# A transformer block on one core: who rotates the first batch's queries and keys

## The chip, the core and the metric

The kernel runs on one core of a Trainium2 chip. The core has a matrix engine (TensorE, PE in the profile; PEld is its weight load), three engines for elementwise work (VectorE or DVE, ScalarE or ACT, GpSimd or POOL), and SyncE (SP), which here issues almost all DMAs. The engines run side by side and wait for each other on semaphores. Each executes its own instructions strictly in the order in which the program holds them. The metric is the device time of one execution in microseconds (us): the median of three runs.

## What is computed

The input is x of 16 batches, 1024 tokens, 256 features. The reference, cut to what matters:

```python
xn = layernorm(x)
Q, K, V = xn @ Wq.T + bq, xn @ Wk.T + bk, xn @ Wv.T + bv      # 16 heads of 16
re, ro = xe * cos - xo * sin, xe * sin + xo * cos             # rotation of Q and K, even and odd columns
attn = softmax(where(causal, Q @ K.T / 4, -1e9)) @ V
h = square(relu(xn @ W_fc.T)); y = h @ W_proj.T
spikes = five steps of a threshold recurrence on y, their sum / 5
out = x + attn @ Wo.T + bo + spikes
```

Products are made from float16 pairs: each operand is split into a high part (a float16 copy) and a low part (what the copy lost, as float16), and a product is three matmuls (high x high, high x low, low x high; `three`, line 590).

## The kernel before, in words

**An order made by a planner.** Every step is announced with `op(engine, cost, when, what, reads, writes, ...)`. `Plan.order` (193 to 321) then plays an event simulation with the given costs and due times `when`: an idle engine takes the ready step that is due first. The resulting order is written down, engine by engine, and a chain of order dependencies fixes it. So a change of an estimated cost, an engine or a dependency in one place can move instructions anywhere later. A step may name other engines in `alt`: if it has been ready and untaken for PATIENCE (1.5 us), an idle engine of that list may take it. `held` names a ring of SBUF tiles (sizes in `BUFS`, line 86); a step is not taken before its tile is free.

**What runs over what.** Batches are 140 us of planned time apart and overlap. For each batch `norms` (595) normalizes the tokens, splits them and transposes them by DMA into xT; `rotated` (655) makes Q and K; `values` (744) makes V; for each of four groups of heads (64 units in all) `largest` (791) takes the row maxima of the scores (matmuls L803, maxima L819 and L837 on VectorE) and `weighted` (910) makes the scores again with the maximum as an extra row (L920), the exponential on ScalarE (L981), the causal mask on POOL (L938) and the product with V (L947); `forward` (1088) is the feed-forward half with its spikes (L1147, L1152) and `projected` (1039) the output. Feed-forward matmuls (L590, with `wfc` and `wproj`) can be placed between attention matmuls. Row-packed matmuls (L803, L920), column-packed ones (L947) and full ones (L590) are three modes between which the planner changes as seldom as its due times allow.

**The rotation, the place of the change.** `rotated` works in four tiles per batch, Q and K of each half of the tokens, each 128 partitions x 1024 float32 (an even and an odd half of 512). A tile passes through these steps:

- two products into PSUM, two biased copies into `r` (`qk`, ScalarE, L670; two buffers),
- `times_` with the sines into `ms`, `times_` with the cosines in place (L678), `added` (L686),
- a float16 copy by ScalarE into `qkhl` (L733), and `less`, the low part (L689),
- `stored`: two DMAs to scratch in DRAM (L693, L697).

`load_slots` later reads Q into `qS` and K into one of three fixed tiles, the slots `kS` (L783). The slots are filled once with a constant by POOL (`memset`, L1232) before the first K is loaded; that fill is made to wait for `st.ready[3]`, the low part of the first batch's last token tile.

The elementwise combinations of two tiles go through `combined` (381). It gives them to POOL, with ScalarE as an alternative where one exists. With `vector=True`, which the first batch's rotation and the low parts of its normalized x (L649) use, VectorE is an alternative without patience, and the estimate for it is 2.1 ns an element. In the first batch the rotation is announced in half tiles (`parts`, `each`), so that the two engines can share a tile.

Of the kernel before, what the change touches and what calls it, by code (L numbers as in the profile page):

```python
# [16 lines left out]
ALU = mybir.AluOpType  # L17
# [4 lines left out]
P = 128  # L22
# [60 lines left out]
Q0, Q1 = 0.1, 0.71  # L83
V0, V1 = 0.43, 0.96
SHARE = 0.5
BUFS = dict(w=5, xn=2, x=3, relu=2, ms=2, hT=3, avT=2, ahl=6)

# [9 lines left out]
FULL, ROWS, COLS = "full", "rows", "cols"  # L97
SWITCH = 100.0
PATIENCE = 1500.0
# [39 lines left out]


class Op:
    __slots__ = ("mode", "engine", "cost", "when", "what", "held", "waits", "then", "start", "early", "ready", "size", "alt", "name", "patience")


class Plan:
# [7 lines left out]
        self.ops, self.writer, self.readers = [], {}, {}  # L153

    def op(self, engine, cost, when, what, reads=(), writes=(), also=(), window=None, size=0.0,
           alt=(), mode=FULL, patience=PATIENCE):
        o = Op()
        o.mode = mode
        o.size, o.alt, o.patience = size, alt, patience
# [24 lines left out]
        for key in writes:  # L184
            k0 = key[0] if isinstance(key, tuple) else key
            if isinstance(k0, (Held, Bank)):
                o.name = k0.name
                break
        for tile_ in held:
            tile_.left += 1  # L190
        self.ops.append(o)

    def order(self):
# [71 lines left out]
        while events:  # L265
            now = events[0][0]
            while events and events[0][0] <= now:
                _, _, kind, o = heappop(events)
                if kind == 0:
                    heappush(queues[o.engine], (o.when, o))  # L270
                    if o.alt:
                        heappush(events, (now + o.patience, n, 3, o))
# [61 lines left out]
def move(nbytes):  # L334
    return nbytes / 360.0
# [23 lines left out]
def tile_block(ctx: ExitStack, tc, x, wqkv, bqk, bv, wo, bo, wfc, wproj, cos, sin, out):  # L359
# [31 lines left out]

    def copied(n, when, out, in_, reads, writes, scale=None):

# [201 lines left out]
    def norms(st, times):  # L595
# [36 lines left out]
        for n in range(NC // 2):  # L632
            i = n // (NC // 4)
            t = times[n]
            if n % (NC // 4) == 0:
                for c in range(HALF):
# [11 lines left out]
            combined(512, t - 2e3,  # L648
                   lambda e, xn=xn, hl=hl: e.tensor_tensor(  # L649
                       hl.t[:, :, 1], xn.t, hl.t[:, :, 0], ALU.subtract),  # L650
                   [xn, (hl, 0)], [(hl, 1)], 2.05, vector=b == 0)
            op("sp", dma(1), t, lambda n=n, hl=hl: turned(n, hl), [(hl, 0), (hl, 1)], [(xT, n)],
               size=2 * move(P * 4 * D * 2))

    def rotated(st, times):
# [16 lines left out]
                bias=bqk_sb[:, 2 * t + eo : 2 * t + eo + 1], scale=1.0 / WS,  # L672
            )


        def times_(engine, table, half, to, r, es):
            cols = slice(half * QB, (half + 1) * QB)
            engine.tensor_tensor(  # L678
                to.t[:, es], r.t[:, es],
                table[:, :, cols].broadcast_to([P, es.stop - es.start, QB]), ALU.mult,  # L680
            )

        def added(engine, r, ms, es):
            for e in range(es.start, es.stop):
                a, b = (r.t[:, e, :], ms.t[:, 1 - e, :])[:: 1 if e == 0 else -1]
                engine.tensor_tensor(r.t[:, e, :], a, b, (ALU.subtract, ALU.add)[e])  # L686

        def less(engine, t, r, hl, es):
            engine.tensor_tensor(hl.t[:, 1 - t, es], r.t[:, es], hl.t[:, t, es], ALU.subtract)  # L689

        def stored(t, half, hl):
            to = scr[b % 2][t][:, :, half * QB : (half + 1) * QB]
# [9 lines left out]
        for half in range(2):  # L702
            for t in range(2):
# [16 lines left out]
                def each(after, what, reads, to, mine, rate=2.27):  # L720
                    for es in parts:
                        own = [(to, e) for e in range(2)[es]]
                        combined(n, at + QD + after, lambda e, es=es: what(e, es),
                                 reads if mine is None else [*reads, *((r, e) for e in range(2)[es])],
                                 own, rate, vector=b == 0)
# [6 lines left out]
                op("act", act(1024), at + QD + 10e3,  # L732
                   lambda t=t, r=r, hl=hl: nc.scalar.copy(hl.t[:, t], r.t), both, [(hl, t, 0), (hl, t, 1)])  # L733
                for es in parts:
# [5 lines left out]
                stored_keys = [(hl, x, e) for x in range(2) for e in range(2)]  # L740
                op("sp", dma(2), at + QD + 13e3, lambda t=t, half=half, hl=hl: stored(t, half, hl),
                   stored_keys, [("scr", b % 2, t, half)], size=move(P * 6 * QB * 2))

    def values(st, times):
        b = st.b
# [475 lines left out]
    for b in range(B):  # L1221
# [5 lines left out]
        if b == 0:  # L1227

            w_fc, WFC = split_weights(wfc, F, "wfc", 2, START + 12e3, [st.ready[1]])
            w_proj, WPROJ = split_weights(wproj, D, "wproj", 2, START + 30e3, [st.ready[3]])  # L1230
            for i, t in enumerate(k_slots):
                op("pool", 1700, START + 40e3 + i, lambda t=t: nc.gpsimd.memset(t, SHIFT),  # L1232
                   [st.ready[3]], [("kS", i)])
        rotated(st, at["q", b])
        values(st, at["v", b])
        for g in range(NG):
# [76 lines left out]
```

## Time and profile before

| | |
|---|---|
| median of 3 runs | 2438.48 us (2437.65 to 2441.66) |
| the profiled execution | 2438.26 us, span of its instructions 2436.6 us |
| TensorE busy | 2356.5 us, 97% |
| VectorE, ScalarE, GpSimd busy | 82%, 76%, 74% |
| mean granted TensorE clock | 0.993 |
| data moved | 246 MB, 101 GB/s |

The span runs from the first to the last instruction. A time of an instruction is its own; an idle time in square brackets stands before it, with what ended it. Matmul ends are modelled, so how fast TensorE gets on is read from the starts. Names after an L are lines of the kernel before.

How the first batch's combinations are spread in the stretch from 20 to 60 us: POOL executes 16 of them in half tiles, VectorE 15, and POOL three fills of 1.8 us each.

### The profile page before, as it was taken

To read this page: it belongs to the slowest core of one execution; us is meant where nothing else is said; L and a number is where in the kernel's file an instruction comes from. 1 tells how busy PE (TensorE), PEld (TensorE's weight loads), DVE (VectorE), ACT (ScalarE), POOL (GpSimd) and SP (SyncE) were. 2 spreads that over 40 slices of the span, in tenths; PEclk is the share of its full clock that TensorE was granted. 3 is DMA by queue.
4 is the path that set the end of the run, shared out by engine and by line. 5 is a ranking of instruction groups with operands and counts; after the bars stand their busy time and mean duration, and the time that the engine had idled before them with its cause. 6 is when DMAs were issued, how large, how long until landed. Compare 5 with 4: busy or idle time off the path is not lost.

```text
span 2436.6 us, 59006 instructions
## 1 busy us (share of the span) xinstructions
PE 2356.5 (97%) x21060; PEld 1182.3 (49%) x21060; DVE 1987.8 (82%) x6065; ACT 1843.3 (76%) x3599; POOL 1806.9 (74%) x1922
## 2 busy tenths in 40 slices
PE   5999999999999999999999999999999999999997
PEld 3544444445445445454544445455454444544553
DVE  6888888887987879788788878877878887787882
ACT  5588778787778778777787777787877878777775
POOL 7877757778678877779778587776877858687553
PEclk8999999999999999999999999999999999999999
DMA  5442524433334344344342434233433242432221
GB/s 170 110 102 80 137 80 120 106 89 108 91 119 111 89 100 109 93 110 123 89 115 84 106 113 105 89 96 84 130 98 115 89 103 88 106 113 82 68 68 54
DMA packets 253935, 246.21 MB, mean 101 GB/s; under 512 B 108104, under 2 KB 207816, under 8 KB 253640
## 3 DMA queue, kind: packets, MB, share of 16 engines
q1 hardware_dynamic: 253504, 242.44, 36.2%
q8 instruction: 165, 2.70, 0.5%
q14 instruction: 130, 1.06, 0.2%
q10 hardware_dynamic: 136, 0.00, 0.0%
HBM read 122.82 MB, written 101.71 MB: 92 GB/s over the span
## 4 chain that ended last, share of the span: by engine, by line
PE 58%; DVE 7%; ACT 3%; issue 2%; DMA 1%; POOL 1%; SPq 0%; POOLq 0%; DVEq 0%; ACTq 0%
PE banks L590 27%; PE banks L947 14%; PE banks L920 8%; PE banks L803 8%; DVE junk L837 3%; ACT w L981 2%; DVE nm_sb L819 1%; DVE count L1152 1%; DVE nm_sb L837 1%; PE banks L1041 1%; PE banks L864 0%; ACT hT L1128 0%; POOL hT L1134 0%; DMA av_dram<-avT 0%; DMA inv<-inv 0%
## 5 line engine op out<-in xcount | busy, mean ns | idle before, releaser
L981 ACT ACTIVATE w<-banks 128x512 f32<-128x512 f32 (+1 forms) x2560 | 1246.6, 572 | 294.6 <-PE banks L920 280.5
L819 DVE TENSOR_REDUCE nm_sb<-banks 128x1 f32<-128x512 f32 x1024 | 642.6, 683 | 138.8 <-PE banks L803 137.6
L947 PE MATMUL banks<-w,v_sb 128*32 128x512 f32 (+3 forms) x6144 | 622.9, 494 | 3.6 <-DVE nm_sb L819 1.4
L938 POOL TENSOR_SCALAR_AFFINE_SELECT w<-w 128x256 f32<-128x256 f32 x1024 | 399.3, 408 | 286.9 <-ACT w L981 271.7
L837 DVE CUSTOM_DVE_ANT_0 junk<-banks,mask,nm_sb 128x256 bf16<-128x256 f32 (+3 forms) x1024 | 498.1, 547 | 99.0 <-PE banks L803 61.9
L837 DVE CUSTOM_DVE_ANT_0 junk<-banks,mask 128x256 bf16<-128x256 f32 (+3 forms) x1024 | 444.4, 486 | 64.0 <-PE banks L803 57.2
L920 PE MATMUL banks<-qS,kS 50*128 50x512 f16 (+3 forms) x3072 | 431.7, 328 | 9.6 <-DVE nm_sb L819 3.5
L803 PE MATMUL banks<-kS,qS 48*128 48x512 f16 (+3 forms) x3072 | 415.8, 326 | 9.5 <-DVE nm_sb L837 4.3
L590 PE MATMUL banks<-wproj_hi,hT 128*128 128x256 f16 x2048 | 383.4, 276 | 8.0 <-ACT relu L1123 6.5
L590 PE MATMUL banks<-xT,wfc_hi 128*128 128x256 f16 x2048 | 350.3, 273 | 6.6 <-ACT w L981 2.5
L590 PEld LDWEIGHTS <-hT 128*128 128x128 f16 x3072 | 282.8, 98 | 110.2 <-issue 74.5
L1130 POOL TENSOR_TENSOR relu<-relu 128x1024 f32<-128x1024 f32 x118 | 223.5, 1894 | 125.6 <-ACT hT L1128 125.1
L920 PEld LDWEIGHTS <-kS 50*128 50x128 f16 x3072 | 132.7, 94 | 314.3 <-issue 288.6
L590 PE MATMUL banks<-wproj_lo,hT 128*128 128x256 f16 x1024 | 281.2, 275 | 0.0
L590 PE MATMUL banks<-xT,wfc_lo 128*128 128x256 f16 x1024 | 279.0, 273 | 0.0
L1134 POOL TENSOR_TENSOR hT<-relu,hT 128x1024 f16<-128x1024 f32 x128 | 273.4, 2136 | 2.9 <-ACT relu L1132 0.9
L947 PEld LDWEIGHTS banks<-w,v_sb 128*32 128x32 f32 x6144 | 152.8, 108 | 245.7 <-issue 189.5
L803 PEld LDWEIGHTS <-qS 48*128 48x128 f16 x3072 | 135.7, 94 | 269.7 <-issue 233.5
L1123 ACT ACTIVATE relu<-banks 128x512 f32<-128x512 f32 x256 | 156.1, 610 | 113.9 <-PE banks L590 110.2
L590 PEld LDWEIGHTS <-wfc_hi 128*128 128x128 f16 x2048 | 185.2, 98 | 92.0 <-issue 70.5
L678 POOL TENSOR_TENSOR ms<-qk,sin_sb 128x1024 f32<-128x1024 f32 (+1 forms) x65 | 150.1, 2309 | 70.5 <-ACT qk L670 70.2
L1152 DVE SCALAR_TENSOR_TENSOR count<-banks,count 128x512 f16<-128x512 f32 x256 | 175.2, 684 | 3.6
(84 smaller groups left out, 2820.7 us busy)
## 6 DMA issues: line engine op xcount, KB each, us to landing
av_dram<-avT SPq DMA_DIRECT2D x128, 256.0 KB, 2.1
qS<-scr_q SPq DMA_DIRECT2D x128, 192.0 KB, 3.5
kS<-scr_k SPq DMA_DIRECT2D x128, 192.0 KB, 4.4
x<-in_x_dram SPq DMA_DIRECT2D x66, 256.0 KB, 3.2
scr_q<-qkhl SPq DMA_DIRECT2D x32, 512.0 KB, 3.1
scr_k<-qkhl SPq DMA_DIRECT2D x32, 512.0 KB, 3.0
av<-av_dram SPq DMA_DIRECT2D x64, 256.0 KB, 3.4
inv<-inv SPq DMA_DIRECT2D x64, 256.0 KB, 3.3
```

The source lines that it names most:

```text
L590: nc.tensor.matmul(out, lhsT=lhs[i], rhs=rhs[j], start=first and n == 0, stop=last and n == 2)
L803: nc.tensor.matmul(pts[two].t[:, at : at + w], lhsT=qS.t[r, h, c * P : (c + 1) * P], rhs=kS[r, h, k0 : k0 + w], start=True, stop=True,)
L819: lambda two=two, pt=pt: nc.vector.tensor_reduce(nm0[:, two, i, c : c + 1], pt.t, axis=AX.X, op=ALU.max),
L837: nc.vector.tensor_tensor_reduce(next(junk)[:, :w], pt.t[:, at : at + w], mask[:, QB - w :], scale=1.0, scalar=nm0[:, two, i, chunk] if pa ...
L920: nc.tensor.matmul(pts[two].t[:, at : at + n], lhsT=kS[r, i, j * P : (j + 1) * P], rhs=qS.t[r, i, qb * QB + off : (qb + 1) * QB], start=Tr ...
L938: nc.gpsimd.affine_select(out=d, in_=d, compare_op=ALU.is_ge, fill=0.0, base=0, pattern=[[0, 2], [1, P]], channel_multiplier=-1,)
L947: nc.tensor.matmul(pav.t[VT * h : VT * (h + 1), off:], lhsT=st.v[:, j, col : col + VT], rhs=ws[h % 2].t[:, h // 2, at : at + QB - off], st ...
L981: lambda n=n, two=two, pt=pt, w=w: nc.scalar.activation(w.t[:, two, :n], pt.t[:, :n], AF.Exp, scale=SCALE),
L1123: lambda r=r, ph=ph, pr=pr: nc.scalar.activation(r.t[:, 2 * pr : 2 * pr + 2].rearrange("p f t -> p (f t)"), ph.t, AF.Relu, scale=1.0 / WS),
L1130: combined(1024, when + 4e3, lambda e, r=r: e.tensor_tensor(r.t, r.t, r.t, ALU.mult), [], [(r, 0), (r, 1)], 1.75, lambda r=r: nc.scalar.ac ...
L1134: lambda e, r=r, hT=hT: e.tensor_tensor(hT.t[:, 1], r.t, hT.t[:, 0], ALU.subtract),
L1152: lambda step=step: nc.vector.scalar_tensor_tensor(flat(count), py.t, least[step], flat(count), ALU.is_gt, ALU.add),
```

## The change

- `combined` takes `vector` as a number. If it isn't 0, the step is VectorE's alone, with an estimate of 70 ns an instruction and 1.06 ns an element; there is no choice left to the planner, and the `patience` field goes.
- The first batch's rotation is announced in whole tiles like that of the others, and goes to VectorE: per tile one product with the sines (1024 elements), one with the cosines, two sums of 512, and one low part of 1024. The low parts of the first batch's normalized x go to VectorE too.
- `ms` loses its entry in `BUFS`, so its ring has one buffer instead of two, in all batches.
- The fill of K's slots waits for `st.ready[1]` instead of `st.ready[3]`: the low part of the second token tile, not of the fourth.

```diff
-BUFS = dict(w=5, xn=2, x=3, relu=2, ms=2, hT=3, avT=2, ahl=6)
+BUFS = dict(w=5, xn=2, x=3, relu=2, hT=3, avT=2, ahl=6)
...
-    def combined(n, when, what, reads, writes, rate=2.27, scalar=None, vector=False):
-        alt, patience = [], PATIENCE
-        if scalar is not None:
-            alt = [("act", act(n) + 35, scalar)]
+    def combined(n, when, what, reads, writes, rate=2.27, scalar=None, vector=0):
         if vector:
-            alt, patience = [("dve", dve(n, 2.1), lambda: what(nc.vector))], 0.0
-        op("pool", pool_(n, rate), when, lambda: what(nc.gpsimd), reads, writes, alt=alt,
-           patience=patience)
+            op("dve", vector * 70 + n * 1.06, when, lambda: what(nc.vector), reads, writes)
+            return
+        alt = [] if scalar is None else [("act", act(n) + 35, scalar)]
+        op("pool", pool_(n, rate), when, lambda: what(nc.gpsimd), reads, writes, alt=alt)
...
-                   [xn, (hl, 0)], [(hl, 1)], 2.05, vector=b == 0)
+                   [xn, (hl, 0)], [(hl, 1)], 2.05, vector=int(b == 0))
...
-                parts = [slice(0, 1), slice(1, 2)] if b == 0 else [slice(0, 2)]
-                n = 1024 // len(parts)
...
-                each(3e3, lambda e, es, half=half, r=r, ms=ms: times_(e, sin_sb, half, ms, r, es),
-                     ["sin"], ms, r)
-                each(5e3, lambda e, es, half=half, r=r: times_(e, cos_sb, half, r, r, es),
-                     ["cos"], r, None)
-                each(8e3, lambda e, es, r=r, ms=ms: added(e, r, ms, es), [(ms, 0), (ms, 1)], r, None)
+                one, two = ((1, 2) if b == 0 else (0, 0))
+                combined(1024, at + QD + 3e3,
+                       lambda e, half=half, r=r, ms=ms: times_(e, sin_sb, half, ms, r),
+                       [*both, "sin"], [ms], vector=one)
+                combined(1024, at + QD + 5e3,
+                       lambda e, half=half, r=r: times_(e, cos_sb, half, r, r), ["cos"], both,
+                       vector=one)
+                combined(1024, at + QD + 8e3, lambda e, r=r, ms=ms: added(e, r, ms), [ms], both,
+                         vector=two)
...
-                for es in parts:
-                    es_ = range(2)[es]
-                    combined(n, at + QD + 12e3,
-                             lambda e, t=t, r=r, hl=hl, es=es: less(e, t, r, hl, es),
-                             [*((r, e) for e in es_), *((hl, t, e) for e in es_)],
-                             [(hl, 1 - t, e) for e in es_], 2.0, vector=b == 0)
+                combined(1024, at + QD + 12e3,
+                       lambda e, t=t, r=r, hl=hl: e.tensor_tensor(
+                           hl.t[:, 1 - t], r.t, hl.t[:, t], ALU.subtract),
+                       [*both, (hl, 0)], [(hl, 1)], 2.0, vector=one)
...
                 op("pool", 1700, START + 40e3 + i, lambda t=t: nc.gpsimd.memset(t, SHIFT),
-                   [st.ready[3]], [("kS", i)])
+                   [st.ready[1]], [("kS", i)])
```

The two programs hold the same matmuls and the same DMAs; their orders differ.

More of the change, by code (lines that the diff above doesn't have):

```diff
@@ L141 @@
 class Op:
-    __slots__ = ("mode", "engine", "cost", "when", "what", "held", "waits", "then", "start", "early", "ready", "size", "alt", "name", "patience")
+    __slots__ = ("mode", "engine", "cost", "when", "what", "held", "waits", "then", "start", "early", "ready", "size", "alt", "name")
 class Plan:
@@ L155, in op @@
     def op(self, engine, cost, when, what, reads=(), writes=(), also=(), window=None, size=0.0,
-           alt=(), mode=FULL, patience=PATIENCE):
+           alt=(), mode=FULL):
         o = Op()
         o.mode = mode
-        o.size, o.alt, o.patience = size, alt, patience
+        o.size, o.alt = size, alt
         o.engine, o.cost, o.when, o.what = engine, cost, when, what
@@ L271, in order @@
                     if o.alt:
-                        heappush(events, (now + o.patience, n, 3, o))
+                        heappush(events, (now + PATIENCE, n, 3, o))
                         n += 1
@@ L673, in biased, with times_, added @@
             )
-        def times_(engine, table, half, to, r, es):
+        def times_(engine, table, half, to, r):
             cols = slice(half * QB, (half + 1) * QB)
             engine.tensor_tensor(
-                to.t[:, es], r.t[:, es],
-                table[:, :, cols].broadcast_to([P, es.stop - es.start, QB]), ALU.mult,
-            )
[L683 to L689, printed above, removed]
+                to.t, r.t, table[:, :, cols].broadcast_to([P, 2, QB]), ALU.mult
+            )
+        def added(engine, r, ms):
+            engine.tensor_tensor(r.t[:, 0, :], r.t[:, 0, :], ms.t[:, 1, :], ALU.subtract)
+            engine.tensor_tensor(r.t[:, 1, :], ms.t[:, 0, :], r.t[:, 1, :], ALU.add)
         def stored(t, half, hl):
@@ L715, in rotated @@
                 both = [(r, 0), (r, 1)]
-                parts = [slice(0, 1), slice(1, 2)] if b == 0 else [slice(0, 2)]
-                n = 1024 // len(parts)
-                def each(after, what, reads, to, mine, rate=2.27):
-                    for es in parts:
[L722 to L725, printed above, removed]
@@ L727, in rotated @@
-                each(3e3, lambda e, es, half=half, r=r, ms=ms: times_(e, sin_sb, half, ms, r, es),
-                     ["sin"], ms, r)
-                each(5e3, lambda e, es, half=half, r=r: times_(e, cos_sb, half, r, r, es),
-                     ["cos"], r, None)
-                each(8e3, lambda e, es, r=r, ms=ms: added(e, r, ms, es), [(ms, 0), (ms, 1)], r, None)
-                op("act", act(1024), at + QD + 10e3,
-                   lambda t=t, r=r, hl=hl: nc.scalar.copy(hl.t[:, t], r.t), both, [(hl, t, 0), (hl, t, 1)])
@@ L734, in rotated @@
-                for es in parts:
-                    es_ = range(2)[es]
-                    combined(n, at + QD + 12e3,
-                             lambda e, t=t, r=r, hl=hl, es=es: less(e, t, r, hl, es),
-                             [*((r, e) for e in es_), *((hl, t, e) for e in es_)],
-                             [(hl, 1 - t, e) for e in es_], 2.0, vector=b == 0)
-                stored_keys = [(hl, x, e) for x in range(2) for e in range(2)]
+                one, two = ((1, 2) if b == 0 else (0, 0))
@@ L741, in rotated @@
+                op("act", act(1024), at + QD + 10e3,
+                   lambda t=t, r=r, hl=hl: nc.scalar.copy(hl.t[:, t], r.t), both, [(hl, 0)])
+                combined(1024, at + QD + 12e3,
+                       lambda e, t=t, r=r, hl=hl: e.tensor_tensor(
+                           hl.t[:, 1 - t], r.t, hl.t[:, t], ALU.subtract),
+                       [*both, (hl, 0)], [(hl, 1)], 2.0, vector=one)
                 op("sp", dma(2), at + QD + 13e3, lambda t=t, half=half, hl=hl: stored(t, half, hl),
-                   stored_keys, [("scr", b % 2, t, half)], size=move(P * 6 * QB * 2))
+                   [(hl, 0), (hl, 1)], [("scr", b % 2, t, half)], size=move(P * 6 * QB * 2))
```

## The prediction

> **What bounds the kernel now.** I read the page's totals first, then the busy time in chosen windows, then the timeline of the first 70 us engine by engine, and last the matmuls of a steady stretch.
>
> ```profile
> span 2436.6 us, 59006 instructions
> ...
> PE 2356.5 (97%) x21060; PEld 1182.3 (49%) x21060; DVE 1987.8 (82%) x6065; ACT 1843.3 (76%) x3599; POOL 1806.9 (74%) x1922
> ```
> ```profile
> 0.00:16.46 16.46, 0.00 (x0) 0.00 (x0) 10.48 (x34) 9.20 (x21) 6.81 (x20) 1.00 0.64 200
> 16.46:33.50 17.04, 17.04 (x102) 10.60 (x103) 11.99 (x18) 10.32 (x16) 12.02 (x8) 1.00 0.69 192
> 33.50:55.50 22.00, 10.70 (x67) 7.30 (x66) 17.27 (x15) 13.29 (x17) 21.86 (x14) 0.79 0.34 116
> 55.50:69.30 13.80, 12.64 (x84) 9.54 (x83) 2.63 (x6) 6.38 (x11) 10.36 (x8) 0.71 0.93 217
> 69.30:120.00 50.70, 48.27 (x368) 27.30 (x368) 49.46 (x156) 26.09 (x45) 47.00 (x34) 1.00 0.41 97
> ...
> 300.00:1200.00 900.00, 889.04 (x8051) 441.57 (x8046) 754.96 (x2344) 702.06 (x1379) 686.82 (x735) 1.00 0.37 102
> ```
>
> Columns: window, its length, busy time of PE, PEld, DVE, ACT, POOL, then granted clock, DMA share, GB/s. From 300 to 1200 TensorE is busy 889 of 900 us: it bounds the body, and what is lost on it earlier stays lost. It loses time only at the start: all of the first 16.46 us, 11.3 of the 22 us up to 55.5 (POOL is busy 21.86 of the 22), and both stretches to 69.3 run at a clock of 0.71 to 0.79. From 69.3 to 120 VectorE is full (49.46 of 50.7).
>
> ```profile
> 32.34 1.80 POOL L1232 MEMSET kS<- 128x2048 f16 x1
> ...
> 39.68 1.70 POOL L678 TENSOR_TENSOR ms<-qk,sin_sb 128x512 f32<-128x512 f32 x1
> ...
> 54.81 1.60 POOL L689 TENSOR_TENSOR qkhl<-qk,qkhl 128x512 f16<-128x512 f32 x1
> ```
> ```profile
> 31.20 1.75 DVE L686 TENSOR_TENSOR qk<-ms,qk 128x512 f32<-128x512 f32 x1
> 32.87 0.68 DVE L678 TENSOR_TENSOR qk<-qk,cos_sb 128x512 f32<-128x512 f32 x1
> 33.47 0.68 DVE L686 TENSOR_TENSOR qk<-qk,ms 128x512 f32<-128x512 f32 x1
> 34.08 1.21 DVE L491 SCALAR_TENSOR_TENSOR wproj_lo<-wproj_stage,wproj_hi 128x1024 f16<-128x1024 f32 x1
> ...
> 36.77 2.28 DVE L491 SCALAR_TENSOR_TENSOR wproj_lo<-wproj_stage,wproj_hi 128x1024 f16<-128x1024 f32 x1
> ```
> ```profile
> 56.44 0.36 SPq L693 DMA_DIRECT2D scr_k<-qkhl  x1
> ...
> 61.48 2.94 SPq L783 DMA_DIRECT2D kS<-scr_k  x4
> ```
> ```profile
> 55.53 0.37 PE L590 MATMUL banks<-wproj_hi,hT 128*128 128x256 f16 x1 [6.46 <-ACT relu L1123]
> ```
>
> A VectorE half tile takes 0.68 us while POOL only fills memory (32.34 to 34.14) and 1.75 while POOL combines as well; a 1024-wide operation takes 1.21 or 2.28. POOL's half tile takes 1.26 alone (its row at 25.32) and 1.70 beside VectorE. So sharing the rotation gives each engine little. The last low part ends at 56.4 (54.81 + 1.60), K is stored, reloaded by 61.48 plus landing, and the first score matmul (L803) starts at 69.33.
>
> **The change part by part.** Each sum is against the profiled execution's 2436.6 us.
>
> *Rotation.* POOL loses 16 half operations (25.8 us in its rows) and VectorE 15 halves; VectorE gets four tiles of sin, cos, two adds and a low part. Starts lie 1.13 us apart for 1024 elements (34.08 to 35.21) and 0.60 for 512 (32.87 to 33.47), so a tile is 3 x 1.13 + 2 x 0.60 = 4.6 us, four are 18.4. VectorE's built order puts among them two wproj_lo (2.3), five statistics pairs of batch 1 (0.56 each by 22.05 to 22.61, 2.8) and two scale pairs (0.6): 24.1 us. The first can start at 24.3, when the second wfc_lo ends (23.14 + 1.21). Without a meeting the last low part ends at 48.4.
>
> *Meetings with POOL.* POOL's built order leaves it, beside these, two rsqrt steps (1.0 each), two low parts of batch 1 (1.15), and relu, hT, relu of the FFN (1.89 + 2.13 + 1.89): 10.2 us. The row at 36.77 paid 2.28 - 1.21 = 1.07 for meeting operations of 1.26, so 0.85 of what it met. Bounds: 0, and 10.2 if all of it lands in VectorE's way. The three FFN operations fall on the last tiles and are met (5.0); of the other 4.3 I take a quarter: 6. The last low part ends at 54.4, 2.0 earlier.
>
> The Trainium skill ("SBUF — State Buffer", Who interferes with whom) speaks against whole tiles: a VectorE instruction with two SBUF inputs and a GpSimd instruction that reads SBUF exclude each other for a whole instruction, though not one that only writes. The two 0.68 rows beside the memset agree with the last part. By the rule all 10.2 us would be paid and the final sum would be 4.2 us worse; the row's price stays.
>
> *SP and the loads.* From K's store to the first score took 69.33 - 56.44 = 12.9 us, with DMA at 0.93 share and 217 GB/s. In the built order SP has moved an x load of 256 KB from between Q's and K's loads to before the stores, and two batch-1 transposes with it: 256 KB at 217 GB/s is 1.2 us. So 11.7 us: 54.4 + 11.7 = 66.1. TensorE's own queue reaches its scores at about the same time: hT of the second half stands on POOL behind a rsqrt that waits for VectorE's last statistics (about 53), so hT at 53 + 1.2 + 2.1 = 56.3, then 12 cold matmuls of 0.213, 48 of 0.109 (24 wproj, 24 wfc), 6 of 0.216: 65.4. First score 66.1, a gain of 3.2 us.
>
> *What TensorE has done by then.* 264 matmuls stand before the first score instead of 252: 24 more 512-wide ones of batch 1 (0.216 each, 5.2 us) and 12 fewer 256-wide ones (0.109, 1.3 us). So 3.9 us of work are ahead. Start in all: -7.1 us; bounds with no meeting and with every one: first score 60.1 and 70.3, so -13.1 and -2.9. VectorE fills the next stretch in both, so I checked it: from the first masked maximum (71.1) to unit 0's maxima being turned (101.9) the before needs 30.8 us; the changed order has two more statistics pairs and two more spike steps there, about 2.5. So 67.9 + 33.3 = 101.2, level, with 8 us more of TensorE work placed before the first exponential: the gain survives.
>
> *K's slots.* Three memsets (5.4 us) leave POOL's full stretch for 14 to 20 us, where POOL idles 6.7 us now: included above. If they came late, the K load would wait for one, 1.8 us.
>
> *Low parts of x.* Two go from POOL to VectorE. The second starts 23.19 and takes 2.17 now; on VectorE some 0.7 from 20.5, so the transpose after it is sooner. TensorE does not wait for it at 29.48: 0; without that cover 4 us would show.
>
> *One ms buffer for all batches.* POOL's order in later batches is sin, cos, add, add, low in both programs, so no sin product waits: 0; if one did, up to a tile's 2.3 us.
>
> *Re-planning.* The built orders differ over the first 53% of TensorE's instructions and are the same, instruction for instruction, after that. In the first part TensorE changes between full, row-packed and column-packed matmuls 30 times less often.
>
> ```profile
> 799.67 0.38 PE L920 MATMUL banks<-qS,kS 50*128 50x512 f16 x2
> 799.88 0.38 PE L803 MATMUL banks<-kS,qS 48*128 48x512 f16 x2
> 800.20 1.06 PE L947 MATMUL banks<-w,v_sb 128*32 128x512 f32 x8
> ```
>
> A pair takes 0.21 us before a pair of the same kind, 0.32 before another kind: 0.11 a change. Eight of the 30 lie before unit 4, where VectorE binds; 22 x 0.11 = -2.4 us (0 to -3.3). Five avT copies go from VectorE to ACT and two squares from POOL to ACT: hidden by ACT's idle quarter, some 5 us over 16 batches if not. The new order's stalls are unknown: TensorE idled 2.4 + 3.8 + 11.0 = 17.2 us from 69.3 to 1200 (the second term is 120 to 300), and I take the same again, with 5 us either way.
>
> Sum: -7.1 - 2.4 = -9.5. Span 2427.1. The profiled run took 2438.26 around its span and the median is 2438.48, so 1.9 is added: 2429.0 us.
>
> **The rivals.**
> 1. *VectorE becomes the start's bound, slower.* The place is the chain of 18 wide VectorE operations. If POOL's next work (batch 1's rotation, 2.3 us each) keeps meeting them, every one costs 2.28 instead of 1.21: 19 us, last low part 67.7, first score 79.4, 10.1 later; less 3.9 of work done and 2.4 of changes, +3.8: 2442. It decides from a first score at 75.6 on (69.3 + 3.9 + 2.4). For it: the 1.75 rows. Against: POOL's list before the last low part holds only 10.2 us.
> 2. *Nothing reaches the end.* VectorE is full up to 120 anyway; if its first-unit stretch starts no sooner and the matmuls done ahead only leave TensorE short of filler later, the 7.1 goes and the 2.4 stays or not: 2437. For it: 49.46 of 50.7. Against: units 0 to 3 hold no more VectorE work than before.
> 3. *The new order stalls more.* If idle over the first half grows from 1.5% to 2.8% of some 1130 us, 15 us: 2444. For it: half of the program stands in an order that no trace shows. Against: fewer changes of kind, and the same work.
>
> **How the numbers follow.** Forecast 0.66, rival 1 0.10, rival 2 0.16, rival 3 0.08. The forecast's own range is 2421 (no meeting, all changes) to 2437 (all meetings, 5 us of stalls); the whole range goes from 2420 to 2440, leaving out most of rivals 1 and 3. About 0.2% (4.9 us, so 2433.6 and 2443.4) is what a measurement here can tell. Faster by more: 0.64, most of the forecast; within: 0.22, rival 2, the weak end of the forecast and part of rival 1; slower: 0.14.
>
> **What would show it.** Right: VectorE's rotation rows near 1.2 us for the first tiles; no POOL rotation before batch 1; memsets before 21; first L803 at 64 to 68; TensorE's idle after 300 still near 1.2%. Wrong: many 1024-wide VectorE rows at 2.2 or more, K's store after 58, a first score after 71, or a first half with clearly more idle.

## The result, and the profile after

The changed kernel takes 2443.85 us (median of 21 runs, 2440.10 to 2450.93), the kernel before 2438.48 (21 runs beside them, 2434.56 to 2443.64): 1.0024 times as long, 95% interval 1.0016 to 1.0031. The forecast was 2429.0, so the sign was wrong. The profiled execution after took 2440.28 us, 3.6 less than its median.

A kernel with the same work in another order, found on the way (experiment 5, estimate 1.2), takes 0.9985 of the time before (0.9976 to 0.9994).

The totals of the page after:

```profile
span 2438.5 us, 59015 instructions
...
PE 2353.6 (97%) x21060; PEld 1184.2 (49%) x21060; DVE 1992.3 (82%) x6066; ACT 1847.5 (76%) x3606; POOL 1777.9 (73%) x1902
```

They show nothing: TensorE's share is the same. The same windows as before (columns: window, length, busy time of PE, PEld, DVE, ACT, POOL, clock, DMA share, GB/s):

```profile
0.00:16.46 16.46, 0.00 (x0) 0.00 (x0) 10.11 (x35) 8.54 (x19) 6.52 (x20) 1.00 0.65 193
16.46:33.50 17.04, 15.26 (x78) 8.42 (x79) 13.79 (x22) 13.76 (x23) 6.47 (x6) 1.00 0.72 198
33.50:55.50 22.00, 15.78 (x102) 10.88 (x102) 21.41 (x25) 12.18 (x18) 11.51 (x6) 0.84 0.65 168
55.50:69.30 13.80, 12.28 (x87) 8.93 (x88) 4.58 (x6) 8.75 (x15) 13.72 (x9) 0.89 0.94 209
69.30:120.00 50.70, 48.46 (x379) 29.78 (x380) 48.36 (x144) 25.17 (x40) 45.83 (x33) 1.00 0.34 87
120.00:300.00 180.00, 174.93 (x1579) 82.07 (x1576) 154.83 (x479) 141.74 (x283) 132.60 (x147) 1.00 0.40 103
300.00:1200.00 900.00, 883.13 (x8005) 442.21 (x8007) 749.15 (x2331) 702.55 (x1381) 676.50 (x730) 1.00 0.37 101
```

From 33.5 to 55.5 the roles are exchanged as announced: VectorE 21.41 us instead of 17.27, POOL 11.51 instead of 21.86, TensorE 15.78 instead of 10.70. The bad news is in the last two rows. From 120 to 300 TensorE is busy 1.3 us less than before (174.93 against 176.19), from 300 to 1200 5.9 us less (883.13 against 889.04). Its idle time from 69.3 to 1200 is 2.2 + 5.1 + 16.9 = 24.2 us, against 17.2 before, the figure that the prediction used. The row from 120 to 300 before:

```profile
120.00:300.00 180.00, 176.19 (x1590) 83.91 (x1587) 157.01 (x481) 145.41 (x289) 141.24 (x153) 1.00 0.41 108
```

VectorE's timeline over the first batch's rotation (L675 sin and cos, L680 and L681 the sums, L721 the low part), and POOL's beside it:

```profile
24.95 1.22 DVE L675 TENSOR_TENSOR ms<-qk,sin_sb 128x1024 f32<-128x1024 f32 x1
...
33.63 2.17 DVE L721 TENSOR_TENSOR qkhl<-qk,qkhl 128x1024 f16<-128x1024 f32 x1
35.73 1.64 DVE L680 TENSOR_TENSOR qk<-qk,ms 128x512 f32<-128x512 f32 x1
37.30 0.68 DVE L681 TENSOR_TENSOR qk<-ms,qk 128x512 f32<-128x512 f32 x1
...
46.66 2.80 DVE L721 TENSOR_TENSOR qkhl<-qk,qkhl 128x1024 f16<-128x1024 f32 x1
49.38 2.61 DVE L680 TENSOR_TENSOR qk<-qk,ms 128x512 f32<-128x512 f32 x1
51.92 2.38 DVE L681 TENSOR_TENSOR qk<-ms,qk 128x512 f32<-128x512 f32 x1
...
55.40 1.22 DVE L721 TENSOR_TENSOR qkhl<-qk,qkhl 128x1024 f16<-128x1024 f32 x1 [0.21 <-ACT qkhl L719]
```
```profile
33.47 3.35 POOL L647 TENSOR_TENSOR xhl<-xn,xhl 128x512 f16<-128x512 f32 x2 [3.10 <-ACT xhl L644]
45.77 2.61 POOL L1113 TENSOR_TENSOR relu<-relu 128x1024 f32<-128x1024 f32 x1 [8.95 <-ACT hT L1111]
48.46 2.99 POOL L1117 TENSOR_TENSOR hT<-relu,hT 128x1024 f16<-128x1024 f32 x1
51.41 2.34 POOL L1113 TENSOR_TENSOR relu<-relu 128x1024 f32<-128x1024 f32 x1
...
56.64 2.12 POOL L1117 TENSOR_TENSOR hT<-relu,hT 128x1024 f16<-128x1024 f32 x1
```

Alone a step takes 1.22 (1024 wide) or 0.68 (512). The five steps beside POOL take 2.17, 1.64, 2.80, 2.61 and 2.38: 0.95 + 0.96 + 1.58 + 1.93 + 1.70 = 7.1 us longer. The last low part ends at 55.40 + 1.22 = 56.6, not at 54.4 as predicted, and K's store and load follow it (SyncE's queue, then TensorE):

```profile
56.65 0.36 SPq L685 DMA_DIRECT2D scr_k<-qkhl  x1
...
61.28 2.88 SPq L766 DMA_DIRECT2D kS<-scr_k  x4
```

The first score, before and after:

```profile
69.33 0.28 PE L803 MATMUL banks<-kS,qS 48*128 48x256 f16 x1
```
```profile
68.42 0.27 PE L786 MATMUL banks<-kS,qS 48*128 48x256 f16 x1 [0.58 <-DMA kS<-scr_k]
```

The first score starts at 68.42 instead of 69.33, with 3.9 us more of matmuls already behind it: 4.8 us ahead. That gain is gone by unit 36.

**Where it goes.** For each kernel the text below uses one quantity worked out from TensorE's rows: at a mark, its start time less the sum of the usual start-to-start spacings (medians by kind) of all matmuls issued before it. That is the time TensorE has lost; the table gives it less the same of the kernel before, each from one profiled execution, and a mark moves by up to half a microsecond with the choice of the usual spacings. "Hands" are the engines that execute the first batch's combinations; an "order" is what a plan gave, PSUM bank numbers included. The rows with an estimate belong to experiments 3 and 5. Marks are the first score and the first weighted sum (L920 before, L903 after) of a unit. It can tell a faster order from one that only does its work in another sequence.

| us lost, against before | first score | unit 4 | unit 20 | unit 36 |
|---|---|---|---|---|
| changed kernel | -4.8 | -2.3 | -1.7 | +6.1 |
| new hands, old order | -2.8 | -0.6 | +0.9 | +1.2 |
| new hands, old order to unit 21, then the new | -1.1 | +0.9 | +1.8 | +10.7 |
| changed, estimate 1.10 | -3.5 | -2.7 | +3.3 | +6.5 |
| changed, estimate 1.2 | -7.2 | -6.9 | -7.3 | -3.6 |
| changed, estimate 2.1 | -2.8 | -0.8 | +12.5 | +24.4 |
| old hands, new order | +2.8 | +6.9 | +7.2 | +16.4 |
| before, one ms buffer alone | +4.0 | +11.0 | +14.0 | +14.0 |
| before, slots filled sooner alone | +3.5 | +9.5 | +6.6 | +9.9 |
| before, planned anew (memset 1600) | +0.3 | -0.3 | +2.0 | +1.8 |

The second row has TensorE's instructions in the order of the kernel before throughout; from unit 4 to 36 it moves by 1.8 us, about what two executions differ by there. Nearer the start they differ by more: two runs of experiment 4 with the changed kernel's order stand at -0.8 and +2.0 at unit 4, where the changed kernel has -2.3, and the second of them at +3.2 at unit 16, where it has -1.7. The table stops at unit 36 because no order of the first six rows differs from that of before behind unit 38 (33 in most of them), and because the profiled execution before lost some 4 us between units 40 and 44 that the one after did not (from 1500 to 1700 us its granted clock is 0.98, after 1.00); so the final spans differ by only 1.9 us while the medians differ by 5.4.

In units 20 to 36 the changed kernel loses 7.8 us. TensorE's waits from 820 to 1400 us show most of it (waiting instruction's line, what it waited for: us in total, times, longest). Before:

```profile
PE banks L590 <- ACT w L981: 1.7, 3, 1.0
PE banks L1041 <- ACT w L981: 0.7, 2, 0.4
PE banks L590 <- DVE nm_sb L837: 0.5, 2, 0.4
...
PE banks L947 <- DVE nm_sb L819: 0.3, 1, 0.3
PE banks L920 <- DVE nm_sb L837: 0.2, 1, 0.2
```

After:

```profile
PE banks L588 <- DVE nm_sb L820: 2.0, 8, 0.3
PE banks L903 <- DVE nm_sb L820: 1.8, 4, 1.1
PE banks L588 <- ACT w L964: 1.6, 2, 1.0
PE banks L903 <- DVE nm_sb L802: 1.1, 3, 0.7
PE banks L786 <- DVE nm_sb L820: 1.0, 3, 0.4
```

Before, VectorE's maxima (`nm_sb`, which read scores out of PSUM) held TensorE up 4 times for 1.0 us; after, 24 times for 7.3 us (all rows with nm_sb added up, the smaller ones too), and all listed waits grow from 4.5 to 11.2 us. The amount of work is the same; the new order has TensorE arrive more often at banks that VectorE has not emptied yet.

### The profile page after: what moved, and what is told of

The parts are those of the page before. It is cut to its first block, busy times and chain, and to the rows that moved or that the text cites. A ratio compares the mean times of both kernels' runs of the same rounds, so it can differ in the third digit from the quotient of the medians.

```text
span 2438.5 us, 59015 instructions
## 1 busy us (share of the span) xinstructions
PE 2353.6 (97%) x21060; PEld 1184.2 (49%) x21060; DVE 1992.3 (82%) x6066; ACT 1847.5 (76%) x3606; POOL 1777.9 (73%) x1902
## 3 DMA queue, kind: packets, MB, share of 16 engines
q14 instruction: 130, 1.06, 0.2%
## 4 chain that ended last, share of the span: by engine, by line
PE 67%; DVE 17%; issue 5%; ACT 5%; DMA 3%; POOL 2%; SPq 1%; POOLq 0%; DVEq 0%; ACTq 0%
PE banks L588 32%; PE banks L930 16%; PE banks L903 9%; PE banks L786 9%; DVE junk L820 7%; DVE nm_sb L802 4%; ACT w L964 3%; DVE count L1135 2%; DVE nm_sb L820 1%; DVE stats L605 1%; PE banks L1024 1%; PE banks L847 1%; DMA xT<-xhl 1%; DVE count L1130 1%; DVE rstd L609 0%
## 5 line engine op out<-in xcount | busy, mean ns | idle before, releaser
L903 PE MATMUL banks<-qS,kS 50*128 50x512 f16 (+3 forms) x3072 | 430.7, 327 | 10.3 <-DVE nm_sb L820 4.0
L903 PEld LDWEIGHTS <-kS 50*128 50x128 f16 x3072 | 133.8, 94 | 312.2 <-issue 284.1
L675 POOL TENSOR_TENSOR ms<-qk,sin_sb 128x1024 f32<-128x1024 f32 x60 | 141.9, 2365 | 65.2 <-ACT qk L668 65.0
```

What stands on the lines that cost most here:

```text
L903: nc.tensor.matmul(pts[two].t[:, at : at + n], lhsT=kS[r, i, j * P : (j + 1) * P], rhs=qS.t[r, i, qb * QB + off : (qb + 1) * QB], start=Tr ...
```

## The experiments

All ratios are to runs of the kernel before on the same chip, five rounds each.

**1. Hands and order apart.** First: the plan of the kernel before, with the first batch's combinations executed whole by VectorE when the second half's turn comes.

```diff
-                   lambda e, xn=xn, hl=hl: e.tensor_tensor(
+                   lambda e, xn=xn, hl=hl: (nc.vector if b == 0 else e).tensor_tensor(
...
+                        seen.append(es)
+                        if len(seen) == 2:
+                            what(nc.vector, slice(0, 2))
```

> The order of the kernel before, instruction for instruction on TensorE, ScalarE and SyncE; only the first batch's rotation and low parts are taken out of POOL's and VectorE's halves and given to VectorE as whole tiles. Theory (the hand-over gains about 5 us at the start, and the loss sits in the re-made order of units 4 to 36, about 11 us): 2438.5 - 5 = 2433 to 2435, and TensorE's lead at the first score matmul stays to the end. Rival (VectorE's whole tiles themselves cost it): 2438.5 or more, up to the changed kernel's 2443.9.

Measured: 2436.41 us, 0.9991 (0.9983 to 1.0000). The reverse: the changed kernel's plan, in which the first batch's tiles are executed in halves by POOL and VectorE side by side, as before.

```diff
+            if b == 0:
+                for e, eng in enumerate((nc.gpsimd, nc.vector)):
+                    eng.tensor_tensor(to.t[:, e], r.t[:, e], table[:, 0, cols], ALU.mult)
+                return
```

> The order of the changed kernel on TensorE, ScalarE and SyncE; in the first batch each rotation step and low part is split again into a half on POOL and a half on VectorE. Theory (order loses about 11, the hand-over gains about 5): 2443.9 + 3 to 6 = 2447 to 2450. Rival (VectorE's whole tiles cost it): back to about 2438.5.

Measured: 2453.22 us, 1.0064 (1.0052 to 1.0076). The first lies between its theory and its rival, the second above both. So the new hands gain in either order: 2.5 us in the old one, where the interval just reaches 1, and 9.4 in the new one (2443.85 against 2453.22). Where the 2.5 us lie isn't shown: in the profile a lead of 2.8 us at the first score is 0.6 by unit 4 and gone by unit 20. With the same hands the new order is slower by 0.33% of the time, 8 us. The loss is the order's.

**2. Two parts alone, in the kernel before.** One `ms` buffer:

```diff
-BUFS = dict(w=5, xn=2, x=3, relu=2, ms=2, hT=3, avT=2, ahl=6)
+BUFS = dict(w=5, xn=2, x=3, relu=2, hT=3, avT=2, ahl=6)
```

> The kernel before with one ms buffer instead of two, nothing else; the planner's order differs over the first third of TensorE's instructions and is the same after it. Theory (any re-made order moves the time by some us, up or down): off 2438.5 by 2 to 8 us, with the difference arising before unit 24. Rival (one buffer makes POOL wait): 2441 to 2444 with a POOL wait that shows. Second rival (nothing matters): within 1 us of 2438.5.

Measured: 2449.44 us, 1.0048 (1.0036 to 1.0060). The slots filled sooner:

```diff
-                   [st.ready[3]], [("kS", i)])
+                   [st.ready[1]], [("kS", i)])
```

> The kernel before with the fill of K's slots waiting for the second token tile instead of the fourth, nothing else; the planner's order differs over the first 60% of TensorE's instructions. Theory: off 2438.5 by 2 to 8 us either way, the start itself about 0 to 3 us sooner. Rival (nothing but the start matters): 2435.5 to 2438.5.

Measured: 2444.30 us, 1.0025 (1.0014 to 1.0035). Both lose nearly everything by unit 4 (+11.0 and +9.5 in the table): with the halves still shared, K's store starts at 60.8 and 59.1 instead of 56.4, and the first score at 75.9 and 71.5 instead of 69.3. Neither part is free on the kernel before; the prediction priced the buffer at 0 and gave the slots no price of their own. With one buffer alone the waits for it that the rival named are there (VectorE's sine product waits 1.16 us for POOL's sum, POOL's 0.26 us for VectorE's) but too short for a store that starts 4.3 us later; the rest is put down to the new plan and not shown.

**3. Another order, and a first attempt at joining two.** One number of the changed kernel's planner altered:

```diff
-            op("dve", vector * 70 + n * 1.06, when, lambda: what(nc.vector), reads, writes)
+            op("dve", vector * 70 + n * 2.1, when, lambda: what(nc.vector), reads, writes)
```

> The changed kernel with one number of its planner altered, the estimated cost of the first batch's six kinds of VectorE steps (2.1 ns an element instead of 1.06): the same instructions on the same engines, a third order that agrees with the changed kernel's in the first 301 and the last 21237 TensorE instructions. Theory (any order planned anew stalls as much or more than the one of before, which was the best of many; the three tried gave +5.4, +5.4 and +10.6 us over before): slower than before by 3 to 10 us, 2442 to 2449, the loss being made at other places than in the changed kernel. Rival (the changed kernel's order is unlucky and the typical re-planned order keeps the start's gain): 2434 to 2437.

Measured: 2458.35 us, 1.0084 (1.0070 to 1.0099), a larger loss than any theory gave, lost all the way from unit 8 to unit 36. Beside it, three kernels that take their order from a table of step numbers instead of the planner:

```diff
-    for o in plan.order():
+    for o in given_order(plan):
```

> The changed kernel's program, instruction for instruction, with its order given as a table: up to the first weighted sum of unit 2 (about 180 us into the span) in the changed kernel's order, from there in the order of the kernel before (both ms buffers kept). Theory (the loss is made by the new order of units 4 to 36; the faster start is real): the changed kernel was 4.8 us ahead at this point in the profile, and nothing later is changed, so 2438.9 - 4.8 = 2434, within 2 us, ratio 0.998. Rival (the start's gain is swallowed by whatever follows, since VectorE is full to 120 us, as the same hands in the old order kept only 0.4 us of 2.8 at unit 0): 2438 to 2440. Second rival (the loss comes from something of the program itself, its number of buffers or banks, and not from the order): 2444.

> The same with the cut at the first weighted sum of unit 20 (about 1000 us): the changed kernel's order up to there, the order of the kernel before behind it. Theory: the changed kernel still stood 1.7 us ahead there by its profile, and the 7.8 us between units 20 and 36 are not paid: 2437, within 2 us. If the loss sits only in units 4 to 20: 2441 or more. If the order is not the cause: 2444.

> The counterpart: the order of the kernel before (with the first batch's rotation and low parts whole on VectorE, as in the run that gave 2436.4) up to the first weighted sum of unit 20, the changed kernel's order from there. Theory (units 20 to 36 in the new order cost 7.8 us by the profile): 2436.4 + 7.8 = 2444, within 2 us. Rival (the later order costs nothing, the 7.8 us are a consequence of what came before): 2436 to 2437.

Measured: 2835.54, 2830.46 and 2845.09 us, 16% above before, whatever the cut. These runs say nothing about the cut. The planner and the table both give a PSUM tile the lowest free bank number. But the planner counts a bank as free only when, in its plan's time, the last reader has finished; the table counted it as free at once behind the last reader's place in the order, so that a tile often got a bank just released. From 300 to 1200 us, then two rows of TensorE's waits over the whole run, of the first of them:

```profile
300.00:1200.00 900.00, 798.89 (x6881) 390.26 (x6878) 652.67 (x2027) 612.93 (x1184) 585.89 (x628) 1.00 0.32 88
```
```profile
PE banks L1104 <- ACT w L1282: 32.6, 71, 0.8
PE banks L1221 <- DVE nm_sb L1138: 27.3, 70, 1.1
```

TensorE is busy 798.89 of 900 us instead of 883.13, and waits some 70 times each, 0.4 to 0.5 us at a time, for a bank's last reader.

**4. Orders joined, with the plans' own banks.** The same, with the bank numbers taken from the plan whose order is used.

> As the first run with an order from a table, with one thing mended: every PSUM bank number now comes from the plan whose order is used (10 tiles around the cut take the bank that was free longest instead); in the run before each tile took the lowest free number, and TensorE waited on banks just released. Up to unit 2's first weighted sum the changed kernel's order, behind it the order of the kernel before. Theory (the new order of units 4 to 36 makes the loss, the faster start is real): 4.8 us below the kernel before, 2434 to 2436, ratio 0.998. Rival (whatever follows swallows the start's gain): 2438 to 2441. Rival (the cause is not the order): 2444.

> The same with the cut at the first weighted sum of unit 6 (about 320 us), where no bank clashes. By the profiles the changed kernel was 2.3 us ahead at unit 4 and 0.3 at unit 8. Theory: the kernel before less 1 to 2 us, 2437 to 2439; if the loss of units 4 to 8 is not one of the order: as the run cut at unit 2.

> The same with the cut at the first weighted sum of unit 18 (about 750 us; one bank changed). The changed kernel was still 1.7 us ahead by its profile: theory 2437 to 2439, so that the rest of the loss (7.8 us) sits behind unit 18. If the loss sits ahead of unit 18: 2442 or more.

Measured: 2446.54 us, 1.0033 (1.0020 to 1.0045); 2444.22, 1.0025 (1.0015 to 1.0035); 2442.83, 1.0021 (1.0012 to 1.0031). The theory's numbers were missed by all three; the last comes out where it was to be if the loss sat ahead of unit 18. Their lost time says why: against before it is -0.8 at unit 4, +3.3 at unit 8 and +4.5 at unit 36 with the cut at unit 6; +3.2 at unit 16, +9.3 at unit 20 and +9.2 at unit 36 with the cut at unit 18; and with the cut at unit 2, -3.2 at the first score, +8.0 at unit 4 and +9.1 at unit 36. Each loses 4 to 11 us within a few units of its own cut, and little in the old order behind that. The two orders stand at different work at a cut, and the passage seems to cost by itself; so these runs do not separate the start's order from the later one. They give one more thing: three further executions of the changed kernel's order of the first 68 us, with lost times at the first score of -3.2, -4.8 and -2.0 (the changed kernel: -4.8).

The counterpart runs the old order with the new hands first and the new order behind unit 21:

> The counterpart with the plans' own banks: the order of the kernel before, the first batch's rotation whole on VectorE, up to the first weighted sum of unit 21 (about 860 us), and the changed kernel's order behind it. Theory (units 20 to 36 cost some 7 us more in the new order): 2436.4 + 7 = 2443, within 2 us. Rival (the later order costs nothing by itself): 2436 to 2438.

Measured: 2445.56 us, 1.0034 (1.0021 to 1.0046). Against the run with the old order throughout (0.9991) it loses 0.43%, 10 us; the theory gave 7, the rival none. Behind the cut it repeats the changed kernel's losses: from unit 20 to 24, 28, 32 and 36 it adds 4.7, 1.7, 1.9 and 0.6 us, the changed kernel 3.3, 1.2, 2.5 and 0.8. So the passage costs little here, and the stretch's order most of it. Its waits from 820 to 1400 have the same form as the changed kernel's (the maxima are L1152 here):

```profile
PE banks L920 <- DVE nm_sb L1152: 2.1, 8, 0.4
PE banks L920 <- ACT w L1296: 1.6, 2, 1.0
PE banks L1235 <- DVE nm_sb L1152: 1.3, 3, 0.9
PE banks L1118 <- DVE nm_sb L1152: 1.0, 3, 0.4
```

6.3 us of them on the maxima, where the same hands in the old order have 1.2. This run has two `ms` buffers, so the single buffer isn't what this stretch pays for. All runs that can be compared over units 20 to 36 (three executions of the new order there, seven of the old one):

| units 20 to 36, us | lost against before | all of TensorE's listed waits | of these for the maxima |
|---|---|---|---|
| old order, seven runs | -1.3 to +1.8 | 3.2 to 5.7 | 0.7 to 1.3 |
| new order: changed kernel | 7.8 | 11.2 | 7.3 |
| new order: old hands | 9.2 | 11.6 | 7.0 |
| new order: joined at unit 21 | 8.9 | 9.7 | 6.3 |
| estimate 1.10 | 3.2 | 7.4 | 6.8 |
| estimate 1.2 | 3.7 | 6.2 | 5.1 |
| estimate 2.1 | 11.9 | 13.0 | 6.8 |

That units 20 to 36 in the new order lose some 8 us, and that the loss is mostly longer waits, is shown. In this order most of the added waits are for VectorE's maxima; but with the estimate 1.10 TensorE waits nearly as long for the maxima and loses 3.2 us, so it is the total of the waits that goes with the loss, not this one kind.

**5. Is it this change, or any new plan?** Two variants of the kernel before with an estimate altered (1600 ns instead of 1700 for a memset; 2.2 ns instead of 2.1 for VectorE's halves):

> The kernel before with one estimate of its planner altered (the memset of a K slot at 1600 ns instead of 1700) and nothing of this change: the same work, the halves still shared out (four of them change sides), and TensorE's order the same in its first 4193 and last 21037 instructions. Theory (the order of before is a lucky or chosen one, and any order planned anew loses): slower by 3 to 15 us, 2441 to 2453. Rival (re-planning is neutral on average, the changed kernel's loss is its own): within 3 us of before, 2436 to 2441.

> The kernel before with another estimate altered (2.2 ns an element instead of 2.1 for VectorE's halves of the first batch; six halves change sides). The same two theories: 2441 to 2453 against 2436 to 2441.

Measured: 2438.98 us, 0.9998 (0.9988 to 1.0008), and 2441.64, 1.0009 (1.0000 to 1.0019). And two changed kernels with 1.10 and 1.2 instead of 1.06 in the line of experiment 3:

> The changed kernel with its estimate of VectorE's first-batch steps at 1.10 ns an element instead of 1.06: the same instructions on the same engines, and an order with 2324 changes of mode and 735 alternations between the two kinds of row-mode work (maxima's scores, weighted sum's scores), against 2325 and 757 in the changed kernel and 2355 and 738 in the one before. Theory that changes and alternations are what an order costs, at 0.11 us each: 23 fewer than the changed kernel, 2443.9 - 2.5 = 2441. Theory that orders scatter by where TensorE runs into waits for banks, whatever these counts: anywhere from 2436 to 2458, and no order with the start's gain kept whole.

> The same with 1.2 ns an element: 2353 changes of mode, 731 alternations, 2 more in all than in the changed kernel. By the counts alone 2444; by scatter anywhere from 2436 to 2458. It would say that the changed kernel's order is only unlucky if this run and the one with 1.10 both fall under 2438.

Measured: 2443.60 us, 1.0020 (1.0011 to 1.0029), and 2435.85, 0.9985 (0.9976 to 0.9994). The theory that any order planned anew loses 3 to 15 us falls with the first and the last (the second stands between the two theories). That the changed kernel's order is only unlucky is not shown either: it was to show in both of the last two under 2438, and one is. The theory that mode changes and alternations set an order's price falls too: the order with the fewest (2324 and 735) is no faster than the changed kernel's (2325 and 757), the one with two more (2353 and 731) is 8 us faster. What stands is scatter: four orders of the same work, all but about four instructions on the same engines, give 2435.85, 2443.60, 2443.85 and 2458.35 us.

The fastest keeps at unit 4 what the prediction had hoped for, -6.9 us. A row of ScalarE and one of TensorE of the changed kernel, then POOL, VectorE, ScalarE, TensorE and a window of the fastest:

```profile
54.32 1.04 ACT L719 CAST qkhl<-qk 128x1024 f16<-128x1024 f32 x1 [3.11 <-DVE qk L681]
55.28 0.59 ACT L1106 ACTIVATE relu<-banks 128x512 f32<-128x512 f32 x1
```
```profile
55.92 0.37 PE L588 MATMUL banks<-wproj_hi,hT 128*128 128x256 f16 x1 [2.81 <-ACT relu L1106]
```
```profile
53.00 2.45 POOL L1117 TENSOR_TENSOR hT<-relu,hT 128x1024 f16<-128x1024 f32 x1
56.90 1.01 POOL L613 TENSOR_TENSOR rstd<-rstd,neg_half 128x4 f32<-128x4 f32 x1 [1.46 <-DVE mr L610]
```
```profile
57.10 1.23 DVE L721 TENSOR_TENSOR qkhl<-qk,qkhl 128x1024 f16<-128x1024 f32 x1 [0.21 <-ACT qkhl L719]
```
```profile
51.25 0.60 ACT L1106 ACTIVATE relu<-banks 128x512 f32<-128x512 f32 x1 [0.68 <-PE banks L588]
```
```profile
55.50 0.39 PE L588 MATMUL banks<-wproj_hi,hT 128*128 128x256 f16 x2 [1.51 <-POOL hT L1117]
```
```profile
55.50:69.30 13.80, 13.19 (x106) 10.38 (x107) 7.50 (x13) 11.44 (x18) 11.97 (x9) 1.00 0.72 183
```

Its last low part ends later than the changed kernel's (58.3 against 56.6), and its first score starts later (70.0). But two steps that feed TensorE come sooner. ScalarE's relu, which empties a bank, runs at 51.25; in the changed kernel it stands behind the copy that waits for VectorE's last sum, and TensorE sits idle 2.81 us for it. And hT, TensorE's next operand, stands in front of the rsqrt instead of behind it and is ready at 55.5 instead of 58.8. So TensorE idles 1.51 us there instead of 2.81, the granted clock of the next window is 1.00 instead of 0.89, it issues 106 matmuls in it instead of 87, and 7.8 us more work than before lies ahead of the first score. That the order of these few steps is worth more here than where the rotation's chain ends is read from these rows; no run altered it alone.

Why one order of units 20 to 36 makes TensorE meet unread banks and another doesn't stays open: no run altered one step of it at a time, and none kept an order and changed its plan's bank numbers alone, except the runs of experiment 3.

## Why the prediction was wrong, point by point

- **The step that failed** is the last term of *Re-planning*: "I take the same again, with 5 us either way". Instead of the 17.2 us of before, TensorE idled 24.2 us from 69.3 to 1200, and by its lost time the new order lost 8.4 us more between units 4 and 36 (-2.3 to +6.1), of it 7.8 behind unit 20. The bound was too narrow as well: over the same stretch the four orders of the changed kernel's work lost 8.4, 9.2, 3.3 and 25.2. None gained, and neither did any other new order in the table. Rival 3 (2444, given 0.08) named this mechanism. That its number is the measured one is luck: it adds 15 us of stalls to the whole forecast, where 8.4 were lost behind unit 4, the start gained less and the mode changes gained nothing. The argument against it, "fewer changes of kind, and the same work", was no argument: the stalls are waits for banks.
- **The -2.4 us for mode changes** gave nothing that shows. The built order has 30 fewer changes between the three modes, but 19 more alternations between the two kinds of row-packed matmuls (738 to 757), which the count left out, although the row quoted as a pair "before a pair of the same kind", L920 before L803, is one. Over units 0 to 36 the fewer changes between the modes lost some 3 us more than before, waits included; in units 20 to 36 the steps from a maxima's score to a weighted sum's score (90 instead of 77) cost 2 to 5 us more, also with their waits and depending on the usual spacing chosen.
- **Rotation**: right. 1.22 and 0.68 a row alone; the first step began at 24.95, 0.6 later than assumed.
- **Meetings**: right in mechanism, mis-sized: 7.1 us instead of 6 of a possible 10.2. With the late start and a wait of 0.2 for ScalarE's copy, the last low part came at 56.6 instead of 54.4. The Trainium skill ("SBUF — State Buffer", Who interferes with whom) has a VectorE instruction with two SBUF inputs and a GpSimd instruction that reads SBUF contend under an exclusive lock. The three FFN steps of POOL agree: VectorE paid 5.2 us for 1.89 + 2.13 + 1.89 = 5.9 of them.
- **SP and the loads**: right, 11.8 us from the last low part to the first score, 11.7 predicted; so 68.42 for 66.1 is the meetings' and the chain's error alone. TensorE's own queue, put at 65.4, ended at 67.8, with hT at 58.8 instead of 56.3; K's load came 0.58 us later.
- **Start in all**: -4.8 instead of -7.1 in this profile, -2.0 to -4.8 in four executions of the order. That 12 more matmuls lie ahead (3.9 us) was right. At unit 4 the lead is -2.3, -0.8 and +2.0 in the three of them that have this order so far.
- **K's slots, the single ms buffer**: in the changed kernel no sine product waited for its buffer and the memsets came early, as said. That they cost nothing holds there only: alone on the kernel before, the run times rise by 0.25% (slots) and 0.48% (buffer), nearly all of it by unit 4.
- **Rival 1** did not happen (first score 68.42, not 75.6). **Rival 2** is half true: with the new hands in the old order 2.8 us at the first score were 0.6 at unit 4. With 1.2 ns as the estimate the start's gain was kept whole up to unit 20 (-7.2, -7.3), so VectorE's fullness doesn't forbid it.
- **The range** doesn't follow exactly from its terms: -13.1 - 3.3 gives 2422, not 2421, and -2.9 - 2.4 + 5 gives 2438, not 2437. That changes nothing here.

## What to carry to other kernels

In a kernel whose order is planned, a change has two effects: what its own steps save, and a new order of everything behind it; here the first was -2.5 us, at the edge of what the runs can tell, and the second +8. The second cannot be read off the diff, and counts of changes did not predict it, so measure the change in the old order as well, and in a few neutral re-plans, before judging it. At a start where TensorE has idle time, look at which steps feed it filler work as well as at the chain to the first score; here the fastest order gained by the former.

## What the runs showed of the hardware

- PSUM bank numbers alone are worth 16%: with the cut at unit 2, the same order on the same engines takes 2835.54 us when a bank is given out again right behind its last reader, and 2446.54 with the plans' own numbers.
- The meeting of VectorE and POOL stretches both: 0.68 to 2.61 for a 512-wide sum, 1.22 to 2.80 for a 1024-wide low part; POOL's hT 2.12 to 2.99, its relu 1.89 to 2.61.
- The same instructions in the same order reach the first score with lost times that differ by 2.8 us (four executions, -2.0 to -4.8), so a gain of that size at a start can't be read from one profile.
